# Planned loads and a two-scalar norm on GpSimd in the last stage of a four-layer graph network

## The chip, the cores and the metric

The kernel runs on one core of a Trainium2 chip. The metric is the device time of one execution in microseconds (us). PE is the matrix engine (PEld its weight loads), DVE the vector engine, ACT the scalar engine, POOL is GpSimd, and SP is the engine that issues the DMAs spoken of here.

## The reference

128 graphs of 128 nodes with 128 features go through four graph layers. Each layer normalises its input over the features, applies a ReLU, runs an attention layer and adds the input back:

```python
def _layernorm(x, axis=-1, eps=1e-5):
    m = jnp.mean(x, axis=axis, keepdims=True)
    v = jnp.var(x, axis=axis, keepdims=True)
    return (x - m) / jnp.sqrt(v + eps)
...
    h = jnp.maximum(_layernorm(x, axis=-1), 0.0)
    x = x + _L0_gnn_ref(h, adj, ...)   # scores from |x_i - x_j|, two norms over the batch
    h = jnp.maximum(_layernorm(x, axis=-1), 0.0)
    x = x + _L1_gnn_ref(h, adj, ...)   # eight heads, masked softmax, then a second attention
    h = jnp.maximum(_layernorm(x, axis=-1), 0.0)
    x = x + _L2_gnn_ref(h, adj, ...)   # one head
    h = jnp.maximum(_layernorm(x, axis=-1), 0.0)
    x = x + _L3_gnn_ref(h, adj, ...)   # scores by edge type, softmax, projection
```

Layer 0 normalises over the whole batch inside, so the kernel first runs through all graphs for it. What is left of layer 0 and all of layers 1 to 3 touch one graph at a time; three of the layernorms above fall into that part.

## The kernel before

The first 1737 us of the profile compute the pair scores and the attention of layer 0 for all graphs; their results (the input plus a bias `xb`, a mask, `y` and `h`) go to device memory. The last stage, `layers_01`, is the version for adjacency values 0 and 1. It works on 32 groups of GC = 4 graphs. A tile called `t` is 128 partitions (nodes or features) x 4 graphs x 128 values in float32.

For each group, `group(g)` is a generator of steps. It takes the four loaded tiles `xg`, `mask`, `yt` and `ht`; ACT scales `yt` into `yl` (L1866), DVE applies a leaky ReLU to it (L551); PE multiplies `ht` and `yl` by the two halves of a weight into `po` (L1872, L1875); DVE adds `xg` and gets `x1` (L1881). Then comes a norm, `normal`: DVE takes statistics (L1669) and aggregates them to mean and variance `mv` (L1671), ACT makes `rs`, one over the root of variance plus eps, with a logarithm and an exponential (L1674, L1675), and POOL makes `xn`, first subtracting the means (L1678) and then multiplying by `rs` (L1679), each time over all four graphs. PE transposes `xn` (`pt`, L1686), ACT applies the ReLU on the way out of PSUM (`hTc`, L1689). Layer 1 follows: PE makes `pf` (L1896), DVE splits it into `f` (L1905 to L1908), ACT makes `f1d` (L1917), PE the head scores `z`, ACT their exponentials (L1776, L1779), DVE bounds and masks them into `p` (L1781), PE sums (L1810), and so on. The norm comes twice more, on `x2` and `x3`, each behind a single-head attention whose DVE steps are L1694 (masking), L1728 and L1721 (the residual). POOL also adds a bias (L1763) and the last residual (L2026); SP then stores the output (L2027).

The order on PE, ACT, DVE and POOL is fixed by a planner, `in_order`. A step says `yield ENGINE, cost, takes, frees`: the engine, its planned time in us, the buffer slots it takes and gives back. `in_order` keeps 8 groups under way, always takes the step that can begin first by these costs, and writes its instructions into the engine's queue. `fork` starts a chain beside the own one, `join` waits for such chains, `done` and `after` name an event and wait for it. The costs only decide the order; on the chip every engine runs its queue strictly in that order and waits for data. SP's queue is not among the four.

Loads were no steps: a group called `load(g + 1)` as it began, which issues the four DMAs in the order `xg`, `mask`, `yt`, `ht` (L1758), and the planner took them to be there at once. Three buffers each hold `xg`, `yt` and `ht`, ten the mask; group 0 was loaded ahead.

Of the kernel before, what the change touches and what calls it, by code (L numbers as in the profile page):

```python
# [15 lines left out]
ALU = mybir.AluOpType  # L16
# [3 lines left out]
P = 128  # L20
# [7 lines left out]
GC = 4  # L28
# [6 lines left out]
Z_T, Z_W, Z_P, Z_F, Z_O, Z_M = 30, 13, 4, 4, 6, 10  # L35
Z_KEPT = {"ps": 1, "t": 4, "w": 2, "v": 1, "vals": 1}
# [20 lines left out]
PE, ACT, DVE, POOL, DMA = "PE", "ACT", "DVE", "POOL", "DMA"  # L57
# [3 lines left out]
AFTER = dict.fromkeys((PE, ACT, DVE, POOL), 0.2) | {DMA: 2.2}  # L61
# [105 lines left out]
def bcast(ap, pos, n):  # L167

    dims = [list(d) for d in ap.ap]
    return bass.AP(tensor=ap.tensor, offset=ap.offset, ap=dims[:pos] + [[0, n]] + dims[pos:])  # L170
# [3 lines left out]
def kernel(ctx: ExitStack, tc: tile.TileContext, x, adj, w, out):  # L174
    nc = tc.nc
    NB = x.shape[0]
# [370 lines left out]
    def inputs_01(g):  # L547
        return xb_d[g], mask_d[g], y_d[g], h_d[g]
# [1080 lines left out]
    def layers_01(first_in):  # L1629

        with tc.tile_pool(name="c_in", bufs=3) as c_in, tc.tile_pool(
# [19 lines left out]
            def tile_t(name):  # L1651
                return c_t.tile([P, GC, P], F32, tag="t", name=name)
# [7 lines left out]
            def tile_s(name, n=GC):  # L1660
                return c_s.tile([P, n], F32, tag="s" + name, name=name)

            def normal(x, out):

                yield DVE, 1.1, "", ""
                s6 = c_s.tile([P, GC, 6], F32, tag="s6", name="s6")
                mv = c_s.tile([P, GC, 2], F32, tag="mv", name="mv")
                for g in range(GC):
                    nc.vector.bn_stats(s6[:, g, :], x[:, g, :])  # L1669
                for g in range(GC):  # L1670
                    nc.vector.bn_aggr(mv[:, g, :], s6[:, g, :])  # L1671
                yield ACT, 0.47, "", ""
                rs = tile_s("rs")
                nc.scalar.activation(rs, mv[:, :, 1], AF.Ln, bias=eps_c)  # L1674
                nc.scalar.activation(rs, rs, AF.Exp, scale=-0.5)  # L1675
                yield POOL, 2.1, "t", ""
                xn = tile_t("xn")
                nc.gpsimd.tensor_tensor(xn, x, bcast(mv[:, :, 0], 2, P), ALU.subtract)  # L1678
                nc.gpsimd.tensor_tensor(xn, xn, bcast(rs, 2, P), ALU.mult)  # L1679
                out.append(xn)  # L1680

            def transposed(xn, out, frees):
# [67 lines left out]
            loaded = dict(first_in)  # L1750

            def load(g):
                tiles = [
                    c_in.tile([P, GC, P], dtype, tag=name, name=name, bufs=n)
                    for name, dtype, n in (("xg", F32, 3), ("mask", BF16, Z_M), ("yt", F32, 3), ("ht", F32, 3))
                ]
                for dst, src in zip(tiles, inputs_01(g)):
                    nc.sync.dma_start(dst, src)  # L1758
                loaded[g] = tiles

            def with_bias3(x3):
                yield POOL, 1.3, "", ""
                nc.gpsimd.tensor_tensor(x3, x3, bcast(pb_bc, 1, GC), ALU.add)  # L1763
# [93 lines left out]

            def group(g):
                b0 = g * GC
                xg, mask, yt, ht = loaded.pop(g)  # L1860
                if g + 1 < NB // GC and g + 1 not in loaded:
                    load(g + 1)
                res = {}
                yield ACT, 0.72, "t", ""
                yl = tile_t("yl")
                nc.scalar.activation(yl, yt, AF.Identity, bias=y_bi, scale=y_sc)  # L1866
                yield DVE, 0.82, "", ""
# [3 lines left out]
                for i in range(GC):  # L1871
# [3 lines left out]
                    nc.tensor.matmul(  # L1875
                        po[:, i, :], yl[:, i, :], wtT[:, 1, :], start=False, stop=i == GC - 1
                    )
                yield "join",
                yield DVE, 0.66, "t", "ps"
                x1 = tile_t("x1")  # L1880
                nc.vector.tensor_tensor(x1, po, xg, ALU.add)  # L1881


                got = []
                yield from normal(x1, got)
                xn = got.pop()
                yield from transposed(xn, got, "")
# [15 lines left out]
                f = c_v.tile([P, 2 * P], BF16, tag="f", name="f")  # L1903
# [57 lines left out]


                yield from normal(x2, got)
                xn = got.pop()
                yield from transposed(xn, got, "")
# [14 lines left out]


                yield from normal(x3, got)
                xn = got.pop()
                yield from transposed(xn, got, "t")
# [41 lines left out]
                nc.gpsimd.tensor_tensor(xh, xh, x3, ALU.add)  # L2026
                nc.sync.dma_start(out_t[:, b0 : b0 + GC, :], xh)  # L2027

            for g in range(2):
                if g not in loaded:  # L2030
                    load(g)
            in_order(
                [partial(group, g) for g in range(NB // GC)], Z_UNDER_WAY,
                {"ps": 4, "pz": 2, "t": Z_T, "w": Z_W, "vals": Z_P, "f": Z_F, "v": Z_O},
                Z_KEPT,
            )

    def layers(simple, first_in):
# [457 lines left out]
    with tc.If(nc.values_load(types[0:1, 0:1]) < 1) as only_01:  # L2496
        layers_01({0: early})
# [42 lines left out]
```

## Time and profile before

| | before |
|---|---|
| median of three runs (lowest, highest) | 2680.19 us (2677.42, 2680.2) |
| profiled execution | 2677.98 us, span 2676.1 us |
| last stage in the profile | from 1737 us to the end, 939 us |
| busy in it: PE, DVE, ACT, POOL | 815.58, 798.38, 718.92, 314.84 us |
| norms on POOL | 96 subtractions and 96 multiplications |

The profiled execution is one of the same program; its 2677.98 us lies 2.2 us under the median. Times in a view of the profile count from the start of its span. A row of a group of instructions reads: line, engine, operation, tiles, shapes, count | busy us, mean ns of one | idle us of the engine before them and who ended it.

### The profile page before, as it was taken

Reading aid. Unit: us, or ns where it says so; the run is one execution under the profiler, and the core shown is the slowest. Engines: PE = TensorE matmul, PEld = TensorE weight load, DVE = VectorE, ACT = ScalarE, POOL = GpSimd, SP = SyncE. Lnnn points to the kernel's source line nnn. Section 1 sums busy time; section 2 is a strip of 40 time slices with the busy share of each in tenths; the row PEclk is TensorE's granted clock in tenths of the full one; section 3 lists DMA queues with packets and bytes.
Section 4 is the critical chain, followed back from the end, with each engine's and each line's share of the span. In section 5 each row is a group of like instructions: output and inputs, shape, how many; then the busy total and the mean of one; then the engine's idle time right before and its main releaser. Section 6 shows DMA issues by size and latency. Waiting matters only on the chain. (4 is left out here: it accounts for less than half of the span.)

```text
span 2676.1 us, 51543 instructions
## 1 busy us (share of the span) xinstructions
PE 2489.0 (93%) x19585; PEld 1559.4 (58%) x19595; DVE 2423.4 (91%) x4638; ACT 2160.1 (81%) x3537; POOL 1632.1 (61%) x922
## 2 busy tenths in 40 slices
PE   8999999999999999799999999778998989898888
PEld 3433444444333333577777777566776767676766
DVE  9999999999999998889998998678988898889886
ACT  8999999999999998466665666468777777787885
POOL 8999999999999999544444443022333333333234
PEclk9999999999999999899999999979998999999999
DMA  3000000000000000322322221040211111110001
GB/s 103 24 24 24 24 24 24 24 24 24 24 24 24 24 23 21 113 86 83 100 92 88 88 84 44 22 133 10 62 35 48 37 37 45 46 45 25 10 2 34
DMA packets 135731, 122.62 MB, mean 46 GB/s; under 512 B 10865, under 2 KB 102450, under 8 KB 135474
## 3 DMA queue, kind: packets, MB, share of 16 engines
q1 hardware_dynamic: 134754, 118.89, 14.6%
q8 instruction: 158, 2.59, 0.4%
q14 instruction: 99, 0.81, 0.1%
q10 hardware_dynamic: 720, 0.33, 0.0%
HBM read 73.05 MB, written 46.14 MB: 45 GB/s over the span
## 5 line engine op out<-in xcount | busy, mean ns | idle before, releaser
L727 POOL TENSOR_TENSOR d<-he 128x2016 f32<-128x2016 f32 (+1 forms) x272 | 961.0, 3560 | 17.7 <-PE ph L752 14.2
L752 PE MATMUL ph<-d,w1T 128*64 128x512 f32 (+1 forms) x4096 | 912.7, 596 | 16.3 <-DVE six L764 9.8
L731 ACT ACTIVATE d<-d 128x2048 f32<-128x2048 f32 (+1 forms) x448 | 833.1, 1888 | 18.0 <-POOL d L727 17.0
L752 PEld LDWEIGHTS ph<-d,w1T 128*64 128x64 f32 x4096 | 322.8, 136 | 545.8 <-issue 471.1
L722 DVE SCALAR_TENSOR_TENSOR d<-pt,he 128x2048 f32<-128x2048 f32 x240 | 543.2, 2271 | 4.6 <-PE ph L752 4.4
L764 DVE BATCH_NORM_STATS2 six<-ph 128x6 f32<-128x512 f32 (+1 forms) x704 | 438.0, 677 | 11.7 <-PE ph L752 11.4
L1678 POOL TENSOR_TENSOR xn<-xo,mv 128x512 f32<-128x512 f32 x64 | 74.0, 1156 | 324.0 <-DVE mv L1671 257.1
L1083 PE MATMUL pl<-its,it 128*128 128x128 f32 x1280 | 171.4, 282 | 2.8 <-DVE its L1076 2.7
L758 ACT ACTIVATE ph<-ph 128x1008 f32<-128x1008 f32 x160 | 159.7, 998 | 11.9 <-PE ph L752 11.6
L1083 PEld LDWEIGHTS pl<-its,it 128*128 128x128 f32 x1280 | 155.5, 194 | 20.7 <-DVE its L1076 7.9
L1781 DVE SCALAR_TENSOR_TENSOR p<-z,mask 128x1024 f32<-128x1024 f32 x124 | 147.7, 1210 | 8.0 <-ACT z L1779 7.7
L1037 ACT ACTIVATE d<-diff 128x640 f32<-128x640 f32 x128 | 89.7, 701 | 79.4 <-PE diff L1028 79.4
L1679 POOL TENSOR_TENSOR xn<-xn,rs 128x512 f32<-128x512 f32 x96 | 110.9, 1155 | 51.3 <-ACT rs L1675 39.5
L1015 POOL TENSOR_TENSOR base<-base,own_d 128x512 f32<-128x512 f32 x32 | 43.4, 1357 | 158.3 <-PE ph L1041 77.4
L1073 ACT CAST it<-pi 128x640 f32<-128x640 bf16 x128 | 86.6, 691 | 64.7 <-PE pi L1070 64.7
L1028 PE MATMUL diff<-inc,h 128*128 128x320 bf16 x768 | 128.6, 304 | 5.8 <-DVE inc L944 3.9
L1779 ACT ACTIVATE z<-z 128x1024 f32<-128x1024 f32 x128 | 129.0, 1008 | 4.1
L944 DVE SCALAR_TENSOR_TENSOR inc<-in_row,row 128x8 bf16<-128x8 f32 (+12 forms) x512 | 126.0, 315 | 1.9 <-PE in_row L935 1.8
L1045 ACT ACTIVATE z<-ph,h_bi,h_sc 128x320 f32<-128x320 f32 x128 | 77.9, 618 | 54.4 <-PE ph L1041 52.5
L1678 POOL TENSOR_TENSOR xn<-x,mv 128x512 f32<-128x512 f32 x32 | 37.0, 1157 | 136.9 <-DVE mv L1671 72.6
L1810 PE MATMUL va<-p,vals 128*32 128x128 f32 x2048 | 107.6, 283 | 8.3 <-DVE vals L1795 4.9
L1076 DVE TENSOR_TENSOR its<-pi,s 128x640 f32<-128x640 bf16 x128 | 102.2, 809 | 13.1 <-ACT it L1073 12.7
(326 smaller groups left out, 5309.3 us busy)
## 6 DMA issues: line engine op xcount, KB each, us to landing
ht<-h SPq DMA_DIRECT2D x64, 256.0 KB, 2.7
n<-ln_xn SPq DMA_DIRECT2D x32, 256.0 KB, 2.4
h<-he SPq DMA_DIRECT2D x32, 256.0 KB, 2.6
adj<-in_adj SPq DMA_DIRECT2D x32, 256.0 KB, 3.0
xn<-n SPq DMA_DIRECT2D x32, 256.0 KB, 2.6
xb<-in_x SPq DMA_DIRECT2D x32, 256.0 KB, 3.0
xb<-xb SPq DMA_DIRECT2D x32, 256.0 KB, 2.0
xg<-xb SPq DMA_DIRECT2D x32, 256.0 KB, 2.7
```

The costliest lines, as they stand in the source:

```text
L722: nc.vector.scalar_tensor_tensor(dv, own, 0.0, later, ALU.max, ALU.max if is_larger else ALU.subtract)
L727: nc.gpsimd.tensor_tensor(dv, later, own, ALU.subtract)
L731: nc.scalar.activation(d[:, 0 : 4 * n], d[:, 0 : 4 * n], AF.Abs, accum_out=sums[:, g, k : k + 1] if on_act else None,)
L752: nc.tensor.matmul(ph[64 * a : 64 * a + 64, t, 0:n], wt, x_, start=part == 0, stop=not is_larger or part == 3,)
L758: nc.scalar.activation(ph[:, :, 0:n], ph[:, :, 0:n], AF.Square, accum_out=squares[:, g, k : k + 1])
L764: nc.vector.bn_stats(six[g][:, 2 * by_bn.index((i, q)) + t, :], ph[:, t, 0:n])
L944: nc.vector.scalar_tensor_tensor(inc[:, :, e : e + n], in_row[:, :, 0:n], float(k + 1), row[:, :, 0:n], ALU.is_equal, ALU.subtract,)
L1028: nc.tensor.matmul(diff[:, a, 0 : SLOT_N // 2], h[:, i, :], inc[:, a * SLOT_N // 2 : (a + 1) * SLOT_N // 2], start=m == 0, stop=m == 2,)
L1083: nc.tensor.matmul(made["pl"][:, i, :], it[:, k, :], its[:, k, :], start=k == 0, stop=k == 4)
L1678: nc.gpsimd.tensor_tensor(xn, x, bcast(mv[:, :, 0], 2, P), ALU.subtract)
L1779: nc.scalar.activation(z, z, AF.Exp, scale=1.0 - SLOPE)
L1781: nc.vector.scalar_tensor_tensor(p, z, 1.0, bcast(mask[:, i, :], 1, NH), ALU.max, ALU.mult)
```

## The change

There are two parts. The norm on POOL becomes one operation for each graph: `tensor_scalar` on 128x128 values, which subtracts the mean and multiplies by `rs`, both given as one value for each partition. Four such instructions take the place of two over four graphs, and the planned cost goes from 2.1 to 1.1. The loads become planned steps on a DMA queue of the planner with a cost of 2.9 and a slot kind `in` of three, given back by the step that makes `x1`; `load(g + 1)` is forked, a group waits in the plan for its own load, the four DMAs are issued in the order `yt`, `ht`, `xg`, `mask`, and the planner begins with ACT busy until 1.5. A `join` ahead of `x1` goes away.

```diff
@@ normal
-                yield POOL, 2.1, "t", ""
+                yield POOL, 1.1, "t", ""
                 xn = tile_t("xn")
-                nc.gpsimd.tensor_tensor(xn, x, bcast(mv[:, :, 0], 2, P), ALU.subtract)
-                nc.gpsimd.tensor_tensor(xn, xn, bcast(rs, 2, P), ALU.mult)
+                for g in range(GC):
+                    nc.gpsimd.tensor_scalar(
+                        xn[:, g, :], x[:, g, :], mv[:, g, 0:1], rs[:, g : g + 1],
+                        ALU.subtract, ALU.mult,
+                    )
@@ load
             def load(g):
+                yield DMA, 2.9, "in", ""
                 tiles = [
...
-                for dst, src in zip(tiles, inputs_01(g)):
-                    nc.sync.dma_start(dst, src)
+                parts = list(zip(tiles, inputs_01(g)))
+                for k in (2, 3, 0, 1):
+                    nc.sync.dma_start(*parts[k])
                 loaded[g] = tiles
+                yield "done", ("loaded", g)
@@ group
-                xg, mask, yt, ht = loaded.pop(g)
-                if g + 1 < NB // GC and g + 1 not in loaded:
-                    load(g + 1)
+                in_slot = "" if g in first_in else "in"
+                if in_slot:
+                    yield "after", ("loaded", g)
+                if g + 1 < NB // GC:
+                    yield "fork", load(g + 1)
                 res = {}
                 yield ACT, 0.72, "t", ""
+                xg, mask, yt, ht = loaded.pop(g)
...
-                yield "join",
-                yield DVE, 0.66, "t", "ps"
+                yield DVE, 0.66, "t", "ps " + in_slot
@@ end of layers_01
-            for g in range(2):
-                if g not in loaded:
-                    load(g)
             in_order(
                 [partial(group, g) for g in range(NB // GC)], Z_UNDER_WAY,
-                {"ps": 4, "pz": 2, "t": Z_T, "w": Z_W, "vals": Z_P, "f": Z_F, "v": Z_O},
-                Z_KEPT,
+                {"ps": 4, "pz": 2, "t": Z_T, "w": Z_W, "vals": Z_P, "f": Z_F, "v": Z_O, "in": 3},
+                Z_KEPT, dict.fromkeys(AFTER, 0.0) | {ACT: 1.5},
             )
```

As the planner decides anew, the order of steps changes on all four engines. At the start of the stage DVE's queue before is four leaky steps, then the first `x1`, one more leaky step and the first statistics; ACT's is eight `yl`, then the first `rs`; PE's is five groups of `po`, then the first `pt`. After the change DVE has one leaky step, the first `x1`, another leaky step, the first statistics; ACT three `yl`, then the first `rs`; PE three groups of `po`, then the first `pt`.

## The prediction

> **What bounds the kernel now.** I read the page's busy table and chain first, then the stage in windows, then its groups of instructions by form, then single instructions in time. The page puts PE and DVE side by side at the top and on the chain:
>
> ```profile
> PE 2489.0 (93%) x19585; PEld 1559.4 (58%) x19595; DVE 2423.4 (91%) x4638; ACT 2160.1 (81%) x3537; POOL 1632.1 (61%) x922
> ...
> PE 13%; DVE 13%; ACT 5%; issue 2%; POOL 0%; DMA 0%; SPq 0%; DVEq 0%; ACTq 0%; POOLq 0%
> ```
>
> Those chain shares are of 2676 us and the chain covers about 35% of it, which is this stage alone: some 356 us of DVE, 359 of PE, 146 of ACT and 6 of POOL's `xn`. The windows say how it begins and runs:
>
> ```profile
> 1737.00:1760.00 23.00, 14.33 (x82) 13.58 (x83) 11.43 (x42) 8.70 (x15) 2.53 (x3) 0.65 0.87 281
> 1760.00:1790.00 30.00, 24.15 (x295) 17.38 (x294) 27.41 (x61) 25.37 (x52) 11.60 (x11) 0.79 0.23 75
> ...
> 2200.00:2300.00 100.00, 91.28 (x992) 73.68 (x991) 85.78 (x193) 78.50 (x173) 34.42 (x32) 0.97 0.16 43
> 2300.00:2400.00 100.00, 87.18 (x932) 66.42 (x932) 88.85 (x196) 80.29 (x173) 36.14 (x33) 0.95 0.13 37
> ```
>
> Columns: window, length, busy PE, PEld, DVE, ACT, POOL, granted clock, DMA share, GB/s. In the first 23 us DVE idles half the time while the DMAs run at 0.87; after that PE and DVE are both near 88%, POOL near 35%. So POOL's own time bounds nothing. What it does to DVE is in the groups of the stage, and in two neighbours in time:
>
> ```profile
> L1679 POOL TENSOR_TENSOR xn<-xn,rs 128x512 f32<-128x512 f32 x96 | 110.9, 1155 | 51.3 <-ACT rs L1675 39.5 <-ACT es L1776 5.7 <-ACT h L1947 0.9
> ...
> L1694 DVE SCALAR_TENSOR_TENSOR p<-p,mask 128x512 f32<-128x512 f32 x62 | 55.7, 900 | 16.0 <-ACT p L1704 15.9
> ...
> L551 DVE SCALAR_TENSOR_TENSOR yl<-yl 128x512 f32<-128x512 f32 x32 | 30.8, 965 | 11.6 <-ACT yl L1866 11.6
> ```
>
> ```profile
> L1694 DVE SCALAR_TENSOR_TENSOR p<-p,mask x62: 649/686/1764, 1827.0 to 2638.7; 128x512 f32<-128x512 f32 x62
> ```
>
> ```profile
> 2624.88 1.04 POOL L1679 TENSOR_TENSOR xn<-xn,rs 128x512 f32<-128x512 f32 x1
> 2624.89 1.58 DVE L1854 SCALAR_TENSOR_TENSOR hv<-xn,hv 128x512 f32<-128x512 f32 x1 [2.26 <-POOL xn L1678]
> ```
>
> The same DVE operation takes 0.65 to 0.69 us or up to 1.76 us (minimum, median, maximum). The long ones begin while a POOL instruction runs, and end about one plain duration after it: 2624.88 + 1.04 + 0.66 is 2626.58, the DVE row ends at 2626.47. DVE instructions that read PSUM show none of this (L1747: 690 to 693 ns). Counted over the stage, as excess over the plain duration of each group (the 30th percentile), 90 DVE instructions lose 58.7 us, every one beside a POOL instruction: 38.5 us beside L1678 and L1679, 20.3 beside L1763 and L2026. Of the 58.7, 26.2 us (45%) lie on the chain.
>
> **Part 1, the norm.** Removed: 192 POOL instructions, 222 us, 1.04 us each when undisturbed. Added: 384 on 128x128. No row has this operation. Nearest in size and inputs is a POOL copy, 128x256 in 402 ns beside a cast of 128x512 in 697 ns: 1.15 ns per column and 107 ns fixed, so 255 ns for 128 columns; the affine select on 128x128 took 292 ns. Dear end: the two-input rows, 3557 ns for 2016 columns and 1040 for 512, give 1.67 ns per column and 183 fixed, so 400 ns. Four are 1.0 to 1.6 us a norm against 2.08 undisturbed; I take 1.15, near the one-input rows, since only one tensor is read. POOL falls from 222 to 110 us.
>
> The Trainium skill's page "GPSIMD Engine Reference", section "Performance pitfalls for Q7 kernels", speaks against four small instructions: a small read command, such as one for a gather's index, costs about 102 cycles and does not overlap the one before. At its 1.2 GHz, two scalars read by each of four instructions would be an estimated 0.68 us a norm on top, 1.83 in all, and the gain of this part about 8 us instead of the 12 below. No row of this profile has such a scalar on POOL, so no run here shows it yet.
>
> The wait on POOL moves: the subtraction could run while ACT made `rs` (rows L1674 296 ns, L1675 206 ns); now the first of the four waits for `rs`. From `mv` to `xn` it was 2.1 to 2.3 us, it becomes about 0.55 + 1.15 = 1.7. So the norm's latency shrinks by 0.5, not by 1.1. Queued behind this wait are the next norm, L1763 and L2026, and behind these the stores on SP; POOL is two thirds idle, which covers it. POOL's 5.9 us on the chain become about 4: gain 2. If that cover were gone, 96 x 0.55 = 53 us of POOL waiting would be the bill.
>
> DVE's stalls beside the norms should fall with POOL's time (110/222) and with the longest single hold (0.28 against 1.04 us): 38.5 x 0.5 x 0.27 = 5, so 33 us of DVE go. At the chain's 45% that is 15 us; PE is as busy as DVE and takes over the chain in part, so I take two thirds: **10 us**. Bounds: 0 (PE's chain hides it all, PE having 816 of 939 us) and 15. The 20 us beside L1763 and L2026 stay.
>
> **Part 2, the loads.** Bytes and buffers are as before, the four DMAs of a load still cost SP about 0.45 us each, and the stores stand behind as many loads in SP's queue to within five (40 in both before the first). As after 1790 us no row shows an engine waiting for a load (all 13.4 us of ACT waiting for `yt` lie before it), in the steady stretch this is worth nothing. The start is different:
>
> ```profile
> ACT yl L1866 <- DMA yt<-y: 13.4, 7, 3.3
> ```
>
> ```profile
> 1757.85 0.28 ACT L1674 ACTIVATE rs<-mv,eps_c 128x4 f32<-128x4 f32 x1
> ...
> 1759.60 1.12 PE L1686 MATMUL pt<-ident,xn 128*128 128x128 f32 x4 [6.05 <-POOL xn L1679]
> ...
> 1772.98 2.35 DVE L1781 SCALAR_TENSOR_TENSOR p<-z,adj 128x1024 f32<-128x1024 f32 x2
> ```
>
> The first `rs` stands behind eight `yl`, each waiting for its DMA, though the first `po` was complete at 1743.0. Walk the new queues with the same rows. `x1` 1743.1; leaky 0.69 and statistics 1.2 to 1745.0; three `yl` are in front of `rs`, the third's `yt` being the fifth transfer instead of the seventh, 384 KB or 1.4 us at 281 GB/s earlier than 1745.4, so 1744.8; `rs` 1745.6; `xn` 1746.8; `pt` behind two more `po` of about 3.2 us each at the half clock seen here, 1750 to 1751. That is 9 us before 1759.6. The same walk (`hTc` 0.6, one `po` 2 to 3, `pf` 0.65, `f` 1.8, two `f1d` blocks of 2.65, `es` and `z` 1.2) puts the first `p` at about 1764 instead of 1773. But less is done before it: DVE 19.0 us (six leaky, four `x1`, four statistics, three `x1h`, three `f`) against 22.5. Lead: 9 - 3.5 = **5.5 us**; bounds 0, if PE's thinner start keeps the clock at the 0.65 of the first window for longer, and 9.
>
> **Order.** All four queues are re-planned. Between windows of 100 us in the steady stretch PE's busy time runs from 86.7 to 91.3 under one plan; a spread of 2.3 over eight such windows, taken as independent, is 2.3 x 2.8 = 6.5 us either way. I take 0 and keep it for the range.
>
> **Sum.** 10 + 2 + 5.5 = 17.5 us: the profiled execution goes from 2677.98 to 2660.5. The median of the runs lies 2.2 us above it, so I forecast 2663.
>
> **Rivals.** About 0.2%, or 5.4 us, is what a measurement of this kernel can tell from no change.
>
> *Hidden (0.13):* DVE's relief goes into waiting for PE, and the early start is spent at a low clock. For it: PE's 88%, clock 0.65 and 0.79 in the first windows. Against: 26 us of the stalls lie on the chain. Time: 2 + 0 to 3 us gained, 2676 to 2680.
>
> *POOL's small instruction is dear (0.10, slower):* nothing bounds it from a row with two scalars. It decides from 0.55 us an instruction: there four cost the 2.2 us of the pair. At 1.0 us a norm takes 4.0, POOL is busy 384 us instead of 222, stalls grow by 384/222 with holds as long as before, 28 us more, 13 of them on the chain; `xn` comes 2 us later, and PEld's 24.5 us of waiting for it grow by a third, 8 us; less the 5.5 at the start, about 16 us slower, 2696. At 0.7 it is about 2684.
>
> *Half of it (0.07):* DVE stays blocked through all four instructions of a norm, so a hold is 1.15 us and stalls only halve. Part 1 gives 5 to 6, the total about 12: 2668.
>
> *As forecast (0.70),* with 4 us less to 15 us more from the bounds and the plan.
>
> **Numbers.** Low end: 15 + 9 + 3 and 7 of luck in the plan, 34 us, 2646. High end: the hidden case and a bad plan, 2682; beyond lies most of the dear instruction. Faster by over 0.2%: forecast 0.70 and half of it 0.07, less 0.04 where the plan is bad, with 0.02 from the hidden case: 0.75. Same 0.14, slower 0.11.
>
> **What would show it.** The POOL row of the new line near 0.25 to 0.4 us, x384; the maximum of L1694's row falling from 1764 to about 1000 or less beside norms, its mean from 900 towards 750; DVE's busy time in the stage down by about 33 us; the first `pt` near 1750 and the first `p` near 1764. A POOL row above 0.55 us, means of DVE's rows unchanged, or a first `p` still near 1773 would make the steps wrong.

## The result and the profile after

| | before | after |
|---|---|---|
| median of six runs each | 2679.31 us | 2720.68 us (2712.87 to 2726.41) |
| ratio, 95% interval | | 1.0157 (1.0145 to 1.017) |
| profiled execution | 2677.98 us | 2716.81 us, span 2715.0 us |

The change costs 41 us. The page of the changed kernel, busy table and chain by line:

```profile
PE 2513.4 (93%) x19595; PEld 1565.5 (58%) x19595; DVE 2387.3 (88%) x4638; ACT 2162.6 (80%) x3537; POOL 1752.6 (65%) x1114
...
PE ph L752 18%; DVE d L722 8%; DVE six L764 6%; POOL xn L1679 6%; PE pl L1083 5%; PE diff L1028 4%; PE ph L1041 3%; PE sp L1051 2%; PE po L1741 2%; PE ph L1948 1%; ACT z L1785 1%; DVE xh L1750 1%; DVE s L1669 1%; PE pp L1837 1%; ACT d L731 1%
```

DVE has 36 us less to do, as was meant, and POOL has 120 us more, which was not. Its `xn` had 6 us of the chain in before; now it has 6% of the span, 163 us. The groups of the stage by form give the new instruction (line, engine, operation, tiles, shapes, count | busy us, mean ns | idle before, by whom it ended):

```profile
L1679 POOL TENSOR_SCALAR xn<-xo,mv,rs 128x128 f32<-128x128 f32 x256 | 226.0, 895 | 278.2 <-ACT rs L1675 173.0 <-ACT es L1782 46.1 <-DVE x L1889 17.2
...
L1697 DVE SCALAR_TENSOR_TENSOR p<-p,mask 128x512 f32<-128x512 f32 x62 | 46.1, 743 | 9.6 <-ACT p L1707 5.4 <-ACT p L1704 3.5 <-ACT es L1782 0.4
...
L551 DVE SCALAR_TENSOR_TENSOR yl<-yl 128x512 f32<-128x512 f32 x31 | 23.9, 772 | 0.9 <-ACT yl L1875 0.9
```

Line 1697 is 1694 of before: its mean falls from 900 to 743 ns, the leaky step's from 965 to 772. The view of POOL's line alone has the undisturbed length (minimum, median, maximum):

```profile
L1679 POOL TENSOR_SCALAR xn<-xo,mv,rs x256: 785/792/2867, 1806.2 to 2690.8; 128x128 f32<-128x128 f32 x128
```

792 ns, four times for each norm. Where nothing is in the way they start 0.77 us apart, which makes 3.1 us a norm; as it ran, the median from the first start to the last end is 3.6 us (3.4 in the kernel priced at 3.3 below). I call it 3.3 us, where the plan has 1.1 and the two old operations took 2.1. Who pays for it is in the list of waits; first the two rows of before, then those of after (who <- for whom: us, times, longest):

```profile
PEld pt L1686 <- POOL xn L1679: 24.5, 19, 6.2
...
PE pt L1686 <- POOL xn L1679: 17.4, 12, 6.0
```

```profile
PEld pt L1689 <- POOL xn L1679: 114.3, 161, 3.6
...
PE pt L1689 <- POOL xn L1679: 74.2, 127, 3.4
```

The two rows of a kernel cover much of the same time (weight load and matmul of one wait), so I compare kernels by the first: 24.5 becomes 114.3 us. What PE itself loses is in the groups of its transposes, before and after (busy us, mean ns | idle before):

```profile
L1686 PE MATMUL pt<-ident,xn 128*128 128x128 f32 x384 | 61.5, 287 | 19.9 <-POOL xn L1679 17.4 <-ACT es L1776 1.6 <-ACT q L2018 0.7
```

```profile
L1689 PE MATMUL pt<-ident,xn 128*128 128x128 f32 x384 | 92.9, 312 | 80.1 <-POOL xn L1679 74.2
```

Busy and idle together are 81 us of PE in before and 173 us after. All other matmuls of the stage were busy 754 us in before (815.58 - 61.5) and 746 after (839.28 - 92.9), so the loss is at the transposes, made good in part by less idle time before other matmuls. PE in order of time in the middle of the stage shows the form of it:

```profile
2440.54 0.48 PE L1689 MATMUL pt<-ident,xn 128*128 128x128 f32 x1 [0.38 <-POOL xn L1679]
2441.32 0.47 PE L1689 MATMUL pt<-ident,xn 128*128 128x128 f32 x1 [0.30 <-POOL xn L1679]
2442.71 0.48 PE L1689 MATMUL pt<-ident,xn 128*128 128x128 f32 x1 [0.92 <-POOL xn L1679]
2443.48 0.48 PE L1689 MATMUL pt<-ident,xn 128*128 128x128 f32 x1 [0.30 <-POOL xn L1679]
```

The transposes have come to the head of PE's queue and go out one by one as POOL finishes each graph. Everything planned behind them stands still. In 40 of the 96 norms the first and the last transpose are over 1.5 us apart, in before in none. The start did what it was to do:

```profile
1745.17 0.38 PE L1689 MATMUL pt<-ident,xn 128*128 128x128 f32 x2
...
1761.67 2.35 DVE L1787 SCALAR_TENSOR_TENSOR p<-z,adj 128x1024 f32<-128x1024 f32 x2
```

The first `p` on DVE is 26.3 us after the stage's first `yl`, where it was 35.0.

### The profile page after: what moved, and what is told of

It is laid out like the page before. It is cut to its first block, busy times and chain, and to the rows that moved or that the text cites. A ratio compares the mean times of both kernels' runs of the same rounds, so it can differ in the third digit from the quotient of the medians.

```text
span 2715.0 us, 51694 instructions
## 1 busy us (share of the span) xinstructions
PE 2513.4 (93%) x19595; PEld 1565.5 (58%) x19595; DVE 2387.3 (88%) x4638; ACT 2162.6 (80%) x3537; POOL 1752.6 (65%) x1114
## 4 chain that ended last, share of the span: by engine, by line
PE 52%; DVE 28%; ACT 9%; POOL 8%; issue 4%; DMA 0%; ACTq 0%; POOLq 0%; DVEq 0%
PE ph L752 18%; DVE d L722 8%; DVE six L764 6%; POOL xn L1679 6%; PE pl L1083 5%; PE diff L1028 4%; PE ph L1041 3%; PE sp L1051 2%; PE po L1741 2%; PE ph L1948 1%; ACT z L1785 1%; DVE xh L1750 1%; DVE s L1669 1%; PE pp L1837 1%; ACT d L731 1%
## 5 line engine op out<-in xcount | busy, mean ns | idle before, releaser
L1679 POOL TENSOR_SCALAR xn<-xo,mv,rs 128x128 f32<-128x128 f32 x256 | 226.0, 895 | 278.2 <-ACT rs L1675 173.0
L1679 POOL TENSOR_SCALAR xn<-x,mv,rs 128x128 f32<-128x128 f32 x128 | 120.5, 953 | 156.7 <-ACT rs L1675 89.3
L1689 PE MATMUL pt<-ident,xn 128*128 128x128 f32 x384 | 92.9, 312 | 80.1 <-POOL xn L1679 74.2
L1689 PEld LDWEIGHTS pt<-ident,xn 128*128 128x128 f32 x384 | 49.8, 145 | 125.0 <-POOL xn L1679 114.3
```

The lines of the kernel that those rows point to most:

```text
L1679: nc.gpsimd.tensor_scalar(xn[:, g, :], x[:, g, :], mv[:, g, 0:1], rs[:, g : g + 1], ALU.subtract, ALU.mult,)
L1689: nc.tensor.transpose(pt[:, g, :], xn[:, g, :], ident)
```

## The experiments

Two things can change in a variant: the order that the planner makes and the instructions that run in it. Where the price of the norm and the loads are the same, the order of instructions on PE, DVE, ACT and SP is the same line for line, whatever POOL runs for the norm. So I name a kernel by its order (loads and price) and its norm ("pair": the two old operations, "four": the four new ones). Medians in us, compared with before in the same job (2675.7 to 2679.3); "single" is one run without an interval.

| order: loads, price | pair | four | other norm |
|---|---|---|---|
| old, 2.1 | before | 2700.6 | |
| old, 1.1 | 2702.0 | 2748.0 | |
| old, 3.3 | | 2711.4 | |
| planned, 1.1 | 2654.8 | after, 2720.7 | one wide: 2644.8 single |
| planned, 2.1 | 2685.7 | | |
| planned, 2.4 | 2670.0 | | |
| planned, 3.0 | | 2658.6 | |
| planned, 3.3 | 2669.4 | 2651.4 | two numbers: 2648.8 single; one scalar: 2661.9 single |
| planned, 3.4 | | 2687.5 | |
| planned, 3.6 | | 2685.3 | |

**The parts, and the price.** The theories were "instruction": 3.3 us a norm cannot be hidden by any order; and "price": the order made with 1.1 puts work ahead of its data. A rival was that the planned loads are to blame.

Planned loads, old norm:

```diff
-                yield POOL, 1.1, "t", ""
+                yield POOL, 2.1, "t", ""
...
-                for g in range(GC):
-                    nc.gpsimd.tensor_scalar(
...
+                nc.gpsimd.tensor_tensor(xn, x, bcast(mv[:, :, 0], 2, P), ALU.subtract)
+                nc.gpsimd.tensor_tensor(xn, xn, bcast(rs, 2, P), ALU.mult)
```

> The planned loads and the new start with the two POOL operations of before and their price of 2.1. Both theories of the loss (dear instruction; wrong price in the plan) lay it on the norm, so both expect the lead of the start here: first p near 1762 to 1764, 5 to 9 us faster than before, about 2671 to 2674. A rival, that the planned loads themselves cost the time, expects 2700 or more.

2685.72 us, ratio 1.0029 (1.0017 to 1.0041). Neither 2671 nor 2700: the lead is there (counted from the first `yl`, the first `p` comes at 23.4 us, almost 12 us earlier, and half of PE's instructions of the stage are done 10 us earlier). It is 7 us when 80% of them are done, 2 us at 90%, and is lost in the last tenth, where the groups run out. The loads are not what costs 41 us, but alone they gave nothing either.

Old loads, new norm and its price, in the kernel before:

```diff
-                yield POOL, 2.1, "t", ""
+                yield POOL, 1.1, "t", ""
...
-                nc.gpsimd.tensor_tensor(xn, x, bcast(mv[:, :, 0], 2, P), ALU.subtract)
-                nc.gpsimd.tensor_tensor(xn, xn, bcast(rs, 2, P), ALU.mult)
+                for g in range(GC):
+                    nc.gpsimd.tensor_scalar(
...
```

> The loads of before; four POOL instructions a norm at the price of 1.1. Both theories of the norm expect the whole loss and the lead of the start missing: 2720 + 5 to 9, so 2722 to 2730. If the loss comes from loads and norm together, it is near 2690.

2748.02 us, ratio 1.0271 (1.025 to 1.0292): worse than expected, so the loss is there without the planned loads. The 27 us between this kernel and the changed one are the difference of two orders.

The changed kernel with the real length as its price:

```diff
-                yield POOL, 1.1, "t", ""
+                yield POOL, 3.3, "t", ""
```

> The changed kernel with the norm priced at 3.3 in the plan, near the 3.4 to 3.5 us that four instructions of 0.79 us and their gaps take. Theory 'price': the queues are then in the order in which data comes, PE's waiting for xn falls from 188 us to about 60, and with the start's lead and the smaller DVE stalls the time is 2660 to 2680. Theory 'instruction': 1.3 us more for each norm cannot be hidden by any order, PE goes on waiting over 130 us for xn, and the time stays at 2705 to 2720.

2651.36 us, ratio 0.9913 (0.9893 to 0.9933): faster than both kernels and than expected, with the same 792 ns instructions. "Instruction" falls as it was put. The waits of this kernel, 41 us in both rows where "price" expected about 60:

```profile
PEld pt L1689 <- POOL xn L1679: 27.0, 47, 1.8
...
PE pt L1689 <- POOL xn L1679: 13.7, 31, 0.8
```

The kernel before with another price and nothing else:

```diff
-                yield POOL, 2.1, "t", ""
+                yield POOL, 1.1, "t", ""
```

> The kernel before with nothing but the norm's price changed from 2.1 to 1.1; the POOL instructions are the old ones and take 2.2 us, so the plan is 1.1 us too early for each norm. Theory 'price': a plan that is too early by about half of what it is in the changed kernel costs about half, 15 to 25 us: 2695 to 2705. Theory 'instruction': the order hardly matters, 2675 to 2687.

2702.03 us, ratio 1.009 (1.0068 to 1.0112), as "price" had it. But this compares two orders, and one could simply be unlucky.

**What makes the instruction long.** One instruction over all four graphs:

```diff
-                for g in range(GC):
-                    nc.gpsimd.tensor_scalar(
-                        xn[:, g, :], x[:, g, :], mv[:, g, 0:1], rs[:, g : g + 1],
-                        ALU.subtract, ALU.mult,
-                    )
+                nc.gpsimd.tensor_scalar(
+                    xn, x, mv[:, 0, 0:1], rs[:, 0:1], ALU.subtract, ALU.mult
+                )
```

> One POOL instruction for a norm over all 512 columns, with the mean and factor of the group's first graph for all four, which leaves out the other graphs' own; only the length of the instruction is read. If the 792 ns are mostly a fixed cost of an instruction with two scalars, it takes about 1.2 us (0.65 fixed, 1.15 ns a column); if they are a cost for each column, about 3.1 us.

And, priced at 3.3, with numbers for both scalars and with a number for one (the two `+` lines are two kernels):

```diff
-                        xn[:, g, :], x[:, g, :], mv[:, g, 0:1], rs[:, g : g + 1],
+                        xn[:, g, :], x[:, g, :], 0.0, 0.1,
+                        xn[:, g, :], x[:, g, :], mv[:, g, 0:1], 0.1,
```

> Four POOL instructions a norm on 128x128 with two fixed numbers in place of the two scalars from memory, which leaves out mean and factor; only the length of the instruction is read. If reading the scalars is what costs, it falls to 0.25 to 0.4 us; if two operations on each column cost it, it stays near 0.79.

> The order made with 3.3; four POOL instructions with the mean from memory and a fixed factor of 0.1, which leaves out the norm's own factor; only the length is read. With two scalars it is 792 ns, with none 642; if each scalar costs the same it is about 717.

POOL's line in the three, wide, numbers, one scalar:

```profile
L1678 POOL TENSOR_SCALAR xn<-xo,mv,rs x64: 2066/2073/3077, 1808.0 to 2617.4; 128x512 f32<-128x512 f32 x64
```

```profile
L1679 POOL TENSOR_SCALAR xn<-xo x256: 642/642/1748, 1806.3 to 2617.4; 128x128 f32<-128x128 f32 x128
```

```profile
L1679 POOL TENSOR_SCALAR xn<-xo,mv x256: 716/717/2244, 1815.3 to 2633.1; 128x128 f32<-128x128 f32 x128
```

From 792 ns at 128 columns to 2073 at 512: 3.34 ns a column and 365 ns fixed. The wide length lies between its two expectations, and so does the one with numbers (0.64 us between 0.4 and 0.79). Each scalar from memory is 75 ns of the 365, and one scalar gives the 717 ns expected. The 3.34 ns are twice the 1.67 a column that the old operations take, as if each of the two operations in the instruction made its own pass. That is argued: no run has this instruction with one operation. So the wide instruction (2.07) costs what the pair cost (2.08), and cutting it in four adds three times 365 ns.

The wide instruction ran on the order of the changed kernel and took 2644.8 us: the same order, a norm 1.2 us shorter, 76 us less (one run).

**Old loads at the right price, and a price a little off.** First the kernel before with four instructions at 3.3, then the changed kernel at 3.6:

```diff
-                yield POOL, 2.1, "t", ""
+                yield POOL, 3.3, "t", ""
...
-                nc.gpsimd.tensor_tensor(xn, x, bcast(mv[:, :, 0], 2, P), ALU.subtract)
-                nc.gpsimd.tensor_tensor(xn, xn, bcast(rs, 2, P), ALU.mult)
+                for g in range(GC):
+                    nc.gpsimd.tensor_scalar(
...
```

```diff
-                yield POOL, 1.1, "t", ""
+                yield POOL, 3.6, "t", ""
```

> The loads of before, four POOL instructions priced at 3.3. If the gain of the rightly priced kernel (25 us) is the smaller DVE stalls, it is mostly here: about 2658 to 2664, the start's lead of 5 to 9 us missing. If the planned loads carry it, the time is near before, 2672 or more.

> The changed kernel with the norm priced at 3.6 instead of 3.3, a little above what it takes. If the gain hangs on a price that is about right, it stays within 8 us of 2651; if 2651 was one lucky order among many, it lies anywhere between 2650 and 2690.

2711.39 us, ratio 1.0127 (1.011 to 1.0144), and 2685.34 us, 1.0025 (1.0013 to 1.0036). The first is far above 2658 to 2664 and 35 us above before as well; the second is outside the 8 us of "price" and inside the range of a lucky order. A right price does not make a good order by itself: 2651 with the planned loads, 2711 with the old ones. Two different orders can't be compared for a cause, so from here on the cause rests on equal ones.

**Equal orders.** The pair on the order of the changed kernel, price left at 1.1:

```diff
                 yield POOL, 1.1, "t", ""
...
-                for g in range(GC):
-                    nc.gpsimd.tensor_scalar(
...
+                nc.gpsimd.tensor_tensor(xn, x, bcast(mv[:, :, 0], 2, P), ALU.subtract)
+                nc.gpsimd.tensor_tensor(xn, xn, bcast(rs, 2, P), ALU.mult)
```

> The changed kernel with its price of 1.1, and so with the same order of instructions on PE, DVE, ACT and SP, but the two old POOL operations, 2.2 us a norm instead of 3.4. If the length of the norm against this order is the cause, the 41 us vanish: 2650 to 2672, PE's waiting for xn back under 60 us. If the order made with 1.1 is bad in itself, it stays above 2700. The DVE stalls come back, 45 to 59 us; against the one wide instruction on the same order (2645, stalls 22) they should cost 10 us or more by the forecast's 45% on the chain.

2654.78 us, ratio 0.9909 (0.9892 to 0.9925): the 41 us vanish, and the order made with 1.1 is not bad in itself. On one and the same order the four instructions cost 2720.7 - 2654.8 = 66 us. Its waits, against 114.3 and 74.2 us:

```profile
PEld pt L1686 <- POOL xn L1679: 30.7, 32, 3.0
...
PE pt L1686 <- POOL xn L1679: 20.5, 21, 2.2
```

Against the wide instruction on this order, with stalls on DVE of some 54 us here and 22 there, the pair is 10 us slower by the times, 7 by the ratios; at least 10 were expected, and the wide one is a single run.

The pair on the order made with 3.3, the same edit with

```diff
-                yield POOL, 1.1, "t", ""
+                yield POOL, 3.3, "t", ""
```

> The order made with 3.3, with the two old POOL operations: the norm is then 1.1 us shorter than planned. On this order 2.6 us instead of 3.3 moved nothing (2649 against 2651). If DVE's stalls matter as forecast, this is 10 to 20 us slower than 2651; if the order alone decides, it is 2645 to 2653.

2669.42 us, ratio 0.9973 (0.9962 to 0.9984). Here the pair is shorter than planned and yet 18 us slower than the four instructions (16 by the ratios), as expected if the stalls matter. What it has more of is stalls on DVE, counted as in the prediction: 49.9 against 21.8 us. The masking line in both:

```profile
L1694 DVE SCALAR_TENSOR_TENSOR p<-p,mask 128x512 f32<-128x512 f32 x62 | 52.2, 845 | 9.7 <-ACT p L1704 7.3 <-ACT p L1701 2.0 <-ACT g L1951 0.3
```

```profile
L1697 DVE SCALAR_TENSOR_TENSOR p<-p,mask 128x512 f32<-128x512 f32 x62 | 46.0, 744 | 10.9 <-ACT p L1707 9.1 <-ACT p L1704 1.5 <-ACT es L1782 0.4
```

The changed kernel at 3.0:

```diff
-                yield POOL, 1.1, "t", ""
+                yield POOL, 3.0, "t", ""
```

> The changed kernel with the norm priced at 3.0. Its measured 3.3 to 3.4 stands between 3.0 and 3.6. If a right price makes the gain, this is a little worse than 2651, 2651 to 2665. If each price draws another order and the draw decides, it lies anywhere between 2645 and 2700.

2658.62 us, ratio 0.9931 (0.9914 to 0.9947): it fits "price" and fits a draw.

Last, four instructions on the order of before:

```diff
                 yield POOL, 2.1, "t", ""
...
-                nc.gpsimd.tensor_tensor(xn, x, bcast(mv[:, :, 0], 2, P), ALU.subtract)
-                nc.gpsimd.tensor_tensor(xn, xn, bcast(rs, 2, P), ALU.mult)
+                for g in range(GC):
+                    nc.gpsimd.tensor_scalar(
...
```

the planned loads with the pair at 2.4, and the changed kernel at 3.4:

```diff
-                yield POOL, 1.1, "t", ""
+                yield POOL, 2.4, "t", ""
...
-                for g in range(GC):
-                    nc.gpsimd.tensor_scalar(
...
+                nc.gpsimd.tensor_tensor(xn, x, bcast(mv[:, :, 0], 2, P), ALU.subtract)
+                nc.gpsimd.tensor_tensor(xn, xn, bcast(rs, 2, P), ALU.mult)
```

```diff
-                yield POOL, 1.1, "t", ""
+                yield POOL, 3.4, "t", ""
```

> The kernel before with its price of 2.1, so with its own order on PE, DVE, ACT and SP, but with the four two-scalar instructions, 3.3 us a norm. If the gap between real and planned length decides, the norm is 1.2 us longer than planned, about as far off as the pair on the order made with 1.1 and the old loads (2702): 2690 to 2710 less some of the 18 us of DVE stalls. If only the order made with 1.1 is sensitive, it is 2660 to 2680.

> The planned loads with the old pair, priced at 2.4 where 2.1 gave 2686. If the planned loads are worth their lead of 9 us at the start, most draws lie below before, 2660 to 2672; if the loads' plan itself is worse, it is at 2680 or more again.

> The changed kernel with the norm priced at 3.4, between 3.3 (2651) and 3.6 (2685). If the price matters through its nearness to the real length, 2648 to 2660; if each price is a draw, anywhere between 2645 and 2690.

2700.56 us, ratio 1.0078 (1.0058 to 1.0098); 2670.03 us, 0.9969 (0.9959 to 0.9979); 2687.54 us, 1.0043 (1.0029 to 1.0057). On the order of before the four instructions cost 24 us (21 by the ratio), with 91.4 us of weight loads waiting for `xn` instead of 24.5; so it is not only the order made with 1.1 that is sensitive. The pair at 2.4 lies where it was expected if the planned loads keep their lead. And 0.1 us of price, 3.3 to 3.4, moves the time by 36 us, as expected of a draw.

## Why the prediction was wrong

**The term that failed is the price of the small instruction.** I took 1.15 us a norm and 1.6 as the dear end; it is 3.3, and POOL went from 222 us to 346, not to 110. Both ends came from rows that make one operation a column; this instruction makes two, and its column costs twice that of the dear rows. The dear end was no bound, since no row of before had two operations or a scalar from memory on POOL. The 107 to 183 ns fixed in those rows are here 365. Of the skill's rule on small reads (page "GPSIMD Engine Reference", section "Performance pitfalls for Q7 kernels") the measured 75 ns for each scalar lies a little under its 102 cycles at 1.2 GHz, an estimated 85 ns; whether it is such a read, no run here shows. My sum by it, 1.83 us, missed the same column cost.

**The rival that came true had its mechanism wrong.** "POOL's small instruction is dear" was there with a chance of 0.10 and a time of 2684 to 2696 for 0.7 to 1.0 us, which is about 2688 at 0.79; it was 2721. It laid 13 us on DVE stalls that grow; they fell from 58.7 to 16.7. It gave PE's waiting 8 us more; the row grew by 90. What was put at nothing is the gap to the plan: the queues are in the order of a norm of 1.1 us, and PE, at 88%, stands behind norms that are over 2 us late. From `mv` to `xn` I had 1.7 us; it is 3.8 at the least and 5.6 in the median, against 2.2 and 2.9 in before. I wrote that POOL "is two thirds idle, which covers it". POOL's idle time did not cover this latency, because PE's queue was ordered for a shorter one. Equal orders show it, four instructions less the pair. The plan lets the norm begin on POOL when `rs` is there. The pair subtracts while ACT still makes `rs`, so undisturbed it needs 1.2 us from `rs` to `xn`, the four 3.2 us; the third column counts from there:

| order | norm's POOL time less its price, four / pair | `rs` to `xn` less the price, four / pair | four less pair |
|---|---|---|---|
| planned loads, 1.1 | 2.2 / 1.0 us | 2.1 / 0.1 us | +66 us |
| old loads, 1.1 | 2.2 / 1.0 us | 2.1 / 0.1 us | +46 us |
| old loads, 2.1 (before) | 1.2 / 0.0 us | 1.1 / -0.9 us | +24 us |
| planned loads, 3.3 | 0.0 / -1.2 us | -0.1 / -2.1 us | -18 us |

The same two sets of instructions go from 66 us worse to 18 us better as the four come less late; by the third column the pair is late on none of these orders. Lateness is not the whole of it: two orders with the same gap differ by 20 us, the wide instruction, 1.1 us late behind `rs` on the order made with 1.1, is the fastest of its three, and the old loads at 3.3 have no run with the pair.

**Part 1, DVE's stalls: right in size by luck, wrong in reason.** The stalls beside the norms fell from 38.5 to 2.2 us (forecast 5), those beside lines 1763 and 2026 of before from 20.3 to 14.6. Their worth is best read where nothing is late, on the order made with 3.3: 18 us, against 10 forecast with bounds 0 and 15; the pair and the wide instruction on the order made with 1.1 give 10. But the reason was not a shorter hold. DVE instructions on 128x512 with two inputs in SBUF that begin inside a norm's POOL instruction took 1139 ns on average in before, 701 after, 731 beside the single wide one of 2.07 us, and 684 alone. It is not the length; a POOL instruction that reads one tensor hardly holds DVE. It is POOL that waits now: in the changed kernel the 241 norm instructions with no such DVE instruction (the 128x1024 `u` counted too) beside them took 790 ns on average, the 47 that began while one ran 1120:

```profile
2303.49 0.68 DVE L1697 SCALAR_TENSOR_TENSOR p<-p,mask 128x512 f32<-128x512 f32 x1
...
2303.51 1.32 POOL L1679 TENSOR_SCALAR xn<-x,mv,rs 128x128 f32<-128x128 f32 x1 [7.30 <-PE sm L1816]
```

**Part 2, the loads: the walk was right, the worth unsteady.** First `pt` 1745.2 (forecast 1750 to 1751), first `p` 1761.7 (1764); 2.6 us of both is that the stage's first `yl` came that much earlier. The `po` were taken at half clock, but the granted clock from 1737 to 1760 was 0.80 instead of 0.65. ACT's waiting for `yt` fell from 13.4 to 3.3 us. Between equal prices the planned loads are worth 27 us (four, 1.1), 47 (pair, 1.1), 60 (four, 3.3) and minus 9 (pair, 2.1), where 5.5 were forecast. These compare different orders, so none of them is the worth of the loads alone.

**Order: the term was too small.** 6.5 us either way came from how much PE's busy time varies between windows of one plan. A step of 0.1 in one price moved the time by 36 us. That term measures the unevenness within one order, not the spread between orders. With it at some 20 us, the chances for faster and slower would have been nearer to each other.

**The sum, by its steps.** The new order and the planned loads, with the pair, are worth 2677.4 - 2654.8 = 23 us; the four instructions on that order take 66 back; the change is slower by 43 by these, 41 measured.

What stays open is why some orders drain badly: the pair at 2.1 and the four instructions at 3.4 and 3.6, all with planned loads, lead before at 80% of PE's instructions (by 7, 18 and 7 us) and are behind it at the end, and no run takes that apart. The granted clock was 0.96 over 1800 to 2500 us in before, 0.94 in the changed kernel and 0.98 in the one priced at 3.3; a PE that stands still more was clocked lower here, and which leads to which was not tried. It can hardly make the 41 us, since the matmuls other than the transposes of `xn` were busy no longer than in before (746 and 754 us).

## What to carry to other kernels

Price a replaced instruction by the operations that it makes on each element, and give its fixed cost once for each piece; here a row with one operation was no bound for an instruction with two. Where a planner fixes the queues, a step that takes longer than its price can cost on the engine that waits in order, however idle its own engine is. Count its length from where the plan lets it begin: the pair looked 1.0 us too long for its price and was not late. The measured length as the price did not make a good order by itself, 2651 us with one set of loads and 2711 with the other. To judge an instruction under such a planner, run both forms on the same order; here two orders differed by up to 36 us from a price changed by 0.1.

## What the runs showed of the hardware

- POOL's two-operation `tensor_scalar` in float32 costs 3.34 ns a column, 215 ns fixed and 75 ns for each scalar from memory (2073, 792, 717 and 642 ns). At 512 columns this one instruction (2.07 us) is no cheaper than two `tensor_tensor` with a broadcast (2.08).
- POOL instructions with one tensor as input barely hold up DVE: 701 to 731 ns against 684, where two-input ones held it to 1139. They wait for DVE themselves: 1120 ns when they begin beside a running DVE instruction with two SBUF inputs, 790 without one. The Trainium skill's page "SBUF — State Buffer", section "Who interferes with whom", says that a DVE instruction with two SBUF inputs contends with a GpSimd instruction that reads SBUF. These runs agree, and show who pays: with two tensors read by POOL, DVE when it comes second (1139 ns) and POOL when it does (1443 ns against 1041 in before); with one tensor POOL alone, and DVE next to nothing.
- The fastest version that computes the whole norm is the changed kernel with one number changed, 3.3 for 1.1: 2651.4 us, 0.9913 of before. The pair on the order made with 1.1, 2654.8 us and 0.9909, can't be told from it.
